# The last 256 tokens before the router: division and projection queued ahead of leftovers, gate logits from unnormalized rows

## The chip, the cores and the metric

The kernel runs on one core of a Trainium2 chip. A core has a matrix engine (TensorE, PE in the profile, with its weight loads as PEld), a vector engine (VectorE, DVE), a scalar engine (ScalarE, ACT), a general engine (GpSimd, POOL) and a queue that only issues transfers (SyncE, SP). Each engine takes its own instructions in the order in which they were queued and waits on semaphores for the others. The metric is the device time of one execution in microseconds (us), here the median of three runs. The profile is that of one further execution.

## The reference: what is computed

Four layers act on x, which holds 4 x 1024 tokens of 256 features. Each is wrapped as `x = x + layernorm(layer(layernorm(x)))`. The first is a gated attention unit with groups of 64 tokens, the second a low-rank feed-forward layer, the third an attention with 16 heads whose weights are `relu(scores)` divided by their row sum, and the fourth a mixture of experts. The change lies where the third ends and the fourth begins:

```python
# third layer, attention
w = relu(q @ k.T / 4);  out = (w / (sum(w) + 1e-6)) @ v
y = x + out @ w_out + b_out          # x here is the normalized input
attn = layernorm(y) * gamma + beta
x = x + layernorm(attn)
# fourth layer, experts: xt is layernorm(x), 4096 rows
S = sigmoid(xt @ Wg).T               # 8 experts x 4096 tokens
G, I = top_k(S, 1024)                # each expert picks its 1024 best tokens
hid = gelu(xt[I] @ W1 + b1)
out = (hid @ W2 + b2) * G            # added back to the chosen rows
```

An expert's choice needs the scores of all 4096 tokens. No expert can begin before the last token has left the attention and has its gate logit.

## The kernel before, in words

Tokens lie in eight blocks `xs[0..7]` of 512 (four tiles of 128 on the partitions). The attention loop (line 1634 on) goes over the batch rows, the query blocks `qh` of 512 tokens, and within these over head groups `g` and key tiles `kt`. For each step `scores` lets PE form `sc` (L1501), ACT and DVE turn it into `w` by a relu (L1509, L1513, L1511, L1517), and two steps later `weigh` lets PE accumulate `po` (L1529). The values carry a column of ones, so `po` holds the row sums too. The very last query block is taken in two halves of 256 tokens (`halves = 2`). The first 256 are called the other quarter below. The second 256 are the last tokens, whose `at_end` is true.

PE, DVE and ACT keep the order in which the program writes their instructions (`manual_schedule`). POOL's and SP's instructions are ordered by the planner of the framework. What follows the scores of a quarter (projection, layer norms, gate) is cut into `Part`s with costs and ages. Those on PE wait in the list `beside`, the others in `rest`, and `next_piece` and `go_on` queue them between the score steps. When the loop is done, four Parts of the other quarter are left. Two are in `rest`: `token_rows` of its two tiles, which normalizes a tile into `hg` (POOL, L1136) and stores `hg` to `tok_d` and x to `x_d` (L1333, L1337). Two are in `beside`: `turn_gating`, which transposes `hg` on PE (L1349) and copies it on ACT (L1352), and `gate`, which multiplies by the gate weights `wgp` (PE, L1364) and adds the result to `logits` (DVE, L1375).

In the kernel before, a loop (L1674) queues these four, and only then line 1683 queues the close of the last tokens, `at_once` (L1391). Its order is as follows. The first half of the projection (`pt`, L1288, channels 0). The transposes of all other tokens' `logits` into `tokens` (L1402). Three idle matmuls (`keep_busy`, L203: their result is not used). The division `by_weight` (DVE, L1257 to L1259) and the transpose `back` into `oT` (L1267). The second half of the projection, which needs `oT`, and 34 idle matmuls. DVE clips the other tokens' logits (L1413), ACT takes their exponential (L1419), and DVE adds the residual into y (L1421). Then there are three sets of moments on DVE with a power on POOL (`moments`, L1384 to L1388), between which y is centred, scaled and added to x (L1424, L1426, L1429, L1431). The normalized rows `hg` (DVE, L1435) are stored and transposed (L1349), copied (ACT, L1352), and multiplied by the gate weights (`pg`, L1364). DVE clips the logits (L1446), PE transposes them (L1449), and ACT takes the exponential (L1450). Meanwhile DVE finishes the sigmoid of the other tokens (L1440, L1441) and SP stores it (L1442).

The small PSUM tiles of this stage (`pt`, `tokens`, `tpg`, `pg`) share three buffers in turn (`side`), so that each new one waits until the third before it has been read.

The expert stage follows. POOL copies the known scores into `by_e` (L1701), DVE finishes the last tokens' sigmoid (L1702, L1703), POOL copies it back (L1704) and SP stores it (L1705). SP loads the bias `mb2` and the weights of two experts (L1707, L1714, L1716). ACT fills a table `each` (L1722) and loads the Gelu table by a tiny activation (L1727). A search for the threshold of expert 0 alternates between DVE (L1755, L1762, L1784, L1787) and PE (L1769). A list of its tokens is built (L1828 to L1918, with `each` read at L1894 and PE's L1904 collecting). POOL gathers the rows from `tok_d` (L1928), PE transposes them (L2098), and from then on PE works without pause on the experts (L2120, L2137).

## Time and profile before

| what | value |
|---|---|
| median of three runs | 1509.32 us (1509.0 to 1512.29) |
| profiled execution, time | 1511.89 us |
| profiled execution, span in the profile | 1510.1 us |
| mean granted PE clock | 0.985 |
| end of the last `po` matmuls | 970.63 us in the span |
| first use of the last tokens' scores (L1702) | 990.12 us |
| first expert matmul (L2120) | 1020.73 us |
| gather of expert 0 (first L1928) | 1015.40 us |

The difference of 1.8 us between time and span lies outside the span. The page of the profile gives, for each engine, its busy time, then its busy tenths in 40 slices of 37.75 us, and the clock that PE was granted. A line of the timeline has the start, the duration, the engine, the source line, the operation, the tile written and the tiles read, the shape, and the number of instructions merged. In brackets stands how long the engine was idle before it and which instruction ended that wait.

### The profile page before, as it was taken

The numbers are of one execution on the slowest core, as the hardware profiler recorded it, in microseconds if no ns is written. First come the engines' busy times: TensorE is split into PE (matmuls) and PEld (weight loads), VectorE is DVE, ScalarE is ACT, GpSimd is POOL, SyncE is SP. The second block draws the span as 40 slices with busy tenths as digits, with TensorE's granted clock in tenths as the row PEclk, the third lists the DMA queues.
The fourth block names the chain that finished last, engine by engine and source line by source line (L and its number), as shares of the span: only waits on it lengthen the run. The fifth ranks groups of instructions, "written<-read, shape, count | busy, mean of one in ns | idle before, by whom it ended". The sixth has DMA issues, their size and how long they took to land. (4 is left out here: it accounts for less than half of the span.)

```text
span 1510.1 us, 24181 instructions
## 1 busy us (share of the span) xinstructions
PE 1461.7 (97%) x9286; PEld 786.1 (52%) x9286; DVE 876.1 (58%) x2140; ACT 698.2 (46%) x1148; POOL 496.5 (33%) x627
## 2 busy tenths in 40 slices
PE   8999999999899999999999999949999999999996
PEld 4666666667532333332333335517666656665674
DVE  5456654666356599659974877775545631322145
ACT  4244455443456666767676788612211122112143
POOL 4123332222350214322432233413334243242554
PEclk9999999999999999999999999969999999999998
DMA  9400000003324141533154210241324324233364
GB/s 219 132 1 1 1 1 1 1 0 101 103 93 144 52 135 60 179 102 102 47 174 140 71 57 30 75 133 34 101 54 92 67 53 98 50 78 81 64 171 122
DMA packets 91885, 121.58 MB, mean 81 GB/s; under 512 B 24925, under 2 KB 64250, under 8 KB 91642
## 3 DMA queue, kind: packets, MB, share of 16 engines
q1 hardware_dynamic: 70000, 73.09, 15.4%
q0 software_dynamic: 21712, 46.94, 13.3%
q8 instruction: 73, 1.20, 0.3%
q14 instruction: 42, 0.34, 0.1%
q10 hardware_dynamic: 58, 0.01, 0.0%
HBM read 66.90 MB, written 53.12 MB: 79 GB/s over the span
## 5 line engine op out<-in xcount | busy, mean ns | idle before, releaser
L1529 PE MATMUL po<-w,vaug 128*17 128x512 f32 (+1 forms) x2304 | 270.1, 551 | 2.8 <-DVE turned L1579 2.6
L2127 ACT ACTIVATE hid<-ph,mb 128x512 f32<-128x512 f32 (+1 forms) x136 | 89.9, 662 | 340.4 <-PE ph L2120 247.8
L2120 PE MATMUL ph<-xT,w 128*128 128x512 f32 (+1 forms) x544 | 229.6, 574 | 0.3 <-DVE xT L2103 0.3
L2137 PE MATMUL py<-w,hid 128*128 128x256 f32 x1024 | 229.7, 380 | 0.0
L2137 PEld LDWEIGHTS py<-w,hid 128*128 128x128 f32 x1024 | 191.7, 190 | 31.7 <-issue 6.7
L1517 DVE TENSOR_SCALAR w<-sc 128x1024 f32<-128x1024 f32 x152 | 185.1, 1222 | 36.2 <-PE sc L1501 33.8
L1509 ACT ACTIVATE w<-sc 128x512 f32<-128x512 f32 x256 | 152.9, 597 | 113.7 <-ACT w L1513 49.5
L1501 PE MATMUL sc<-q,kT 32*128 32x512 f32 (+1 forms) x2304 | 190.8, 413 | 2.2 <-ACT w L1509 1.0
L1501 PEld LDWEIGHTS sc<-q,kT 32*128 32x128 f32 x2304 | 86.2, 183 | 174.7 <-ACT w L1509 92.1
L2158 POOL DMA_INDIRECT acc_d<-y,idx x56 | 88.8, 1586 | 225.2 <-DVE y L2157 103.2
L2120 PEld LDWEIGHTS ph<-xT,w 128*128 128x128 f32 x544 | 99.8, 190 | 107.4 <-issue 98.3
L1513 ACT ACTIVATE w<-sc 128x512 f32<-128x512 f32 x203 | 120.2, 592 | 0.0
L1515 ACT ACTIVATE w<-sc 128x1024 f32<-128x1024 f32 x104 | 106.7, 1026 | 0.0
L2156 DVE TENSOR_TENSOR y<-py,mb 128x256 f32<-128x256 f32 x56 | 23.5, 420 | 126.7 <-PE py L2137 116.1
L1529 PEld LDWEIGHTS po<-w,vaug 128*17 128x17 f32 x2304 | 41.7, 95 | 95.8 <-issue 72.3
L1928 POOL DMA_INDIRECT got<-tok_d,idx x64 | 66.6, 1041 | 62.9 <-DVE counts L1762 24.5
L2103 DVE COPY xT<-tp 128x512 f32<-128x512 f32 (+1 forms) x34 | 22.2, 659 | 71.1 <-PE tp L2098 62.4
L724 PE MATMUL pg<-nT,wh 128*128 128x512 f32 x128 | 61.4, 612 | 1.5 <-ACT nT L663 1.5
L850 PE MATMUL py<-wo,oT 128*128 128x256 f32 x256 | 61.9, 385 | 0.0
L740 PE MATMUL pv<-wh,nT 128*128 128x512 f32 x128 | 59.7, 592 | 0.0
L850 PEld LDWEIGHTS py<-wo,oT 128*128 128x128 f32 x256 | 47.2, 190 | 17.2 <-issue 9.6
L915 ACT ACTIVATE hid<-ph,vec 128x512 f32<-128x512 f32 x64 | 39.8, 685 | 27.5 <-PE ph L906 27.4
(309 smaller groups left out, 2108.8 us busy)
## 6 DMA issues: line engine op xcount, KB each, us to landing
q<-q_d POOLq DMA_DIRECT2D x16, 1024.0 KB
w<-in_L_ffn_W_dram SPq DMA_DIRECT2D x16, 1024.0 KB
q_d<-parts SPq DMA_DIRECT2D x48, 256.0 KB
kT<-k_d POOLq DMA_DIRECT2D x16, 512.0 KB
k_d<-parts SPq DMA_DIRECT2D x24, 256.0 KB
acc_d<-logits SPq DMA_DIRECT2D x8, 512.0 KB
tok_d<-hg SPq DMA_DIRECT2D x32, 128.0 KB
x<-in_L_attn_x_dram SPq DMA_DIRECT2D x7, 512.0 KB
```

Source lines behind the costliest of these rows:

```text
L850: nc.tensor.matmul(py, lhsT=d["oT"][:, e, :], rhs=wo[:, e, :], start=(e == 0), stop=(e == EC - 1))
L1501: nc.tensor.matmul(sc[:, m * n : (m + 1) * n], lhsT=row["kT"][t][rows, r, (kt + m) * P : (kt + m + 1) * P], rhs=row["q"][qh, t][rows, r, p ...
L1509: nc.scalar.activation(w[:, 0, :], singles[0], AF.Relu)
L1513: nc.scalar.activation(w[:, 1, :], singles[1], AF.Relu)
L1515: nc.scalar.activation(w[:, 2:4, :], pair, AF.Relu)
L1517: nc.vector.tensor_scalar(w[:, 2:4, :], pair, 0.0, None, ALU.max)
L1529: nc.tensor.matmul(po[32 * j : 32 * j + HD + 1, weighed(halves, r)], lhsT=row["v"][:, kt + m, HQ * t + 4 * r + j, :], rhs=w[:, j, m * n : ...
L1928: return nc.gpsimd.indirect_dma_start(out=dst, out_offset=None, in_=rows[:, :], in_offset=self.at_chunk(c), bounds_check=NT - 1, oob_is_er ...
L2120: nc.tensor.matmul(ph, lhsT=w1[:, c, f * P : (f + 1) * P], rhs=xT[u][:, c, h * n : (h + 1) * n], start=(c == 0), stop=(c == DC - 1),)
L2127: nc.scalar.activation(hid[:, f, h * n : (h + 1) * n], ph, AF.Gelu, bias=mb1[:, e * FC + f : e * FC + f + 1])
L2137: nc.tensor.matmul(py, lhsT=hid[:, f, i * P : (i + 1) * P], rhs=w2[:, f, :], start=(f == 0), stop=(f == FC - 1),)
L2158: scatter = nc.gpsimd.indirect_dma_start(out=acc_d[:, :], out_offset=lists[e].at_chunk(k), in_=y, in_offset=None, bounds_check=NT - 1, oob ...
```

## The change

1. The loop that queued the leftovers becomes a function `go_on_down_to(n)`, which is handed to `at_once`. It is called with 1 behind the division and the transpose of the last tokens (this queues both `token_rows` and `turn_gating` of the other quarter), and with 0 behind the first set of moments (this queues its `gate`). So the first half of the projection stands in PE's queue ahead of the other quarter's transposes, and the division stands in DVE's queue ahead of the other quarter's logit sum.
2. The transposes of the other tokens' logits, the clip and the exponential move behind that. The idle matmuls change from 3 and 34 to 2 and 20, and their places change.
3. The gate of the last tokens no longer takes the normalized rows. x itself is transposed and multiplied by the gate weights, and ACT copies the product out. A matmul of a tile of ones with the gate weights gives the column sums of the weights on every partition (`of_gate`). After the transposes of the logits, DVE forms `(of_gate * mean - logit) * rs`, clips it at 87 and hands it to the exponential, now without a scale of -1. This is the logit of the normalized rows with its sign turned.
4. The normalized rows are still written to `tok_d`, but POOL forms them, and they are queued behind the exponential.
5. `each` and the Gelu table are made to wait for the last exponential.

```diff
@@ -1339,15 +1339,16 @@
             def token_rows_and_on(i, rs, ms):
                 token_rows(i, lambda dst, src: scaled(dst, src, rs, ms))
 
-            def turn_gating(i0):
+            def turn_gating(i0, of=None):
                 if i0 == tiles[0]:
                     new_turn([] if at_end else [*turns, gates])
                     gating["hT"] = wk.tile([P, DC, TB], F32, tag="hT", name="hTg")
+                of = gating["h"] if of is None else of
                 tp = side([P, DC, 2, P], "tpg")
                 for c in range(DC):
                     for i in range(2):
                         nc.tensor.transpose(
-                            tp[:, c, i, :], gating["h"][:, i0 + i, c * P : (c + 1) * P], ident
+                            tp[:, c, i, :], of[:, i0 + i, c * P : (c + 1) * P], ident
                         )
                 nc.scalar.copy(
                     gating["hT"][:, :, i0 * P : (i0 + 2) * P], tp.rearrange("p c i t -> p c (i t)")
@@ -1388,68 +1389,80 @@
                     nc.gpsimd.tensor_tensor(rs[:, :, 0], ve[:, :, 0], mhalf[:, 0:2], ALU.pow)
                 return [(i, mv[:, k, 0:1], rs[:, k, :]) for k, i in enumerate(tiles)]
 
-            def at_once(by_weight, back):
+            def at_once(by_weight, back, go_on_down_to):
 
 
                 new_y()
                 x, stt = xs[t], nc.vector.scalar_tensor_tensor
+                k_tiles = SEG // P
                 pts = [(i, side([P, D], "pt")) for i in tiles]
                 for i, pt in pts:
                     project_tile(pt, i, (0,))
-                idle = ps.tile([P, 2, TB], F32, tag="d", name="idle", bufs=2)[:, 0, :]
-                tokens = side([P, SEG // P, P], "tokens")
-                for k in range(SEG // P):
-                    nc.tensor.transpose(tokens[:, k, :], logits[:, k * P : (k + 1) * P], ident)
-                keep_busy(idle, 3)
                 by_weight()
                 back()
+                go_on_down_to(1)
                 for i, pt in pts:
                     project_tile(pt, i, (1,))
-                keep_busy(idle, 34)
-
-
-                for k in range(SEG // P):
-
-                    nc.vector.tensor_scalar(
-                        score_t.rearrange("p (b z k) e -> p k z b e", b=B, k=SEG // P)[:, k],
-                        tokens[:, k, :].rearrange("p (z b e) -> p z b e", b=B, e=NE),
-                        -87.0, None, ALU.max,
-                    )
-                known = score_t[:, 0 : NTILE - SEG // P]
-                nc.scalar.activation(known, known, AF.Exp, scale=-1.0)
+
+                idle, psum = (ps.tile([P, 2, TB], F32, tag="d", name=name, bufs=2)[:, 0, :] for name in ("idle", "psum"))
+                ones = wk.tile([P, P], F32, tag="parts", name="ones")
+                nc.gpsimd.memset(ones, 1.0)
+                of_gate = wk.tile([P, NE], F32, tag="parts", name="of_gate")
+                keep_busy(idle, 2)
                 for i, pt in pts:
                     nc.vector.tensor_tensor(y[:, i, :], pt, h[:, i, :], ALU.add)
                 scales = moments("b", y, "take")
+                go_on_down_to(0)
+                tokens = side([P, k_tiles, P], "tokens")
+                for k in range(k_tiles):
+                    nc.tensor.transpose(tokens[:, k, :], logits[:, k * P : (k + 1) * P], ident)
+                for c in range(DC):
+                    nc.tensor.matmul(psum[:, 0:NE], lhsT=ones, rhs=wgp[:, c, 0, 0:NE], start=(c == 0), stop=(c == DC - 1))
+                nc.scalar.copy(of_gate, psum[:, 0:NE])
+                keep_busy(idle, 20)
                 for i, mean, rs in scales:
                     stt(y[:, i, :], y[:, i, :], mean, gam, ALU.subtract, ALU.mult)
                 for i, mean, rs in scales:
                     stt(y[:, i, :], y[:, i, :], rs, bet, ALU.mult, ALU.add)
                 scales = moments("c", y, "take")
+
+                for k in range(k_tiles):
+
+                    nc.vector.tensor_scalar(
+                        score_t.rearrange("p (b z k) e -> p k z b e", b=B, k=k_tiles)[:, k],
+                        tokens[:, k, :].rearrange("p (z b e) -> p z b e", b=B, e=NE),
+                        -87.0, None, ALU.max,
+                    )
+                known = score_t[:, 0 : NTILE - k_tiles]
+                nc.scalar.activation(known, known, AF.Exp, scale=-1.0)
                 for i, mean, rs in scales:
                     nc.vector.tensor_scalar(y[:, i, :], y[:, i, :], mean, None, ALU.subtract)
                 for i, mean, rs in scales:
                     stt(x[:, i, :], y[:, i, :], rs, x[:, i, :], ALU.mult, ALU.add)
-                for i, mean, rs in moments("g", x, "take"):
+                turn_gating(tiles[0], x)
+                pg, rows = gate()
+                scales = moments("g", x, "take")
+                nc.vector.tensor_scalar(known, known, 1.0, None, ALU.add)
+                nc.vector.reciprocal(known, known)
+                nc.sync.dma_start(score_rows[:, 0 : NTILE - k_tiles], known)
+                last_logits = wk.tile([P, SEG], F32, tag="hT", name="last_logits")
+                nc.scalar.copy(last_logits[rows, :], pg[rows, :])
+                tokens = side([P, k_tiles, 32], "tokens")
+                for k in range(k_tiles):
+                    nc.tensor.transpose(tokens[:, k, :], last_logits[rows, k * P : (k + 1) * P], ident[rows, rows])
+                at = wk.tile([P, k_tiles, NE], F32, tag="even", name="at", bufs=1)
+                for k, (i, mean, rs) in enumerate(scales):
+                    stt(at[:, k, :], of_gate, mean, tokens[:, k, 32 - NE : 32], ALU.mult, ALU.subtract)
+                for k, (i, mean, rs) in enumerate(scales):
+                    nc.vector.tensor_scalar(at[:, k, :], at[:, k, :], rs, 87.0, ALU.mult, ALU.min)
+                state["exp"] = nc.scalar.activation(score_t[:, NTILE - k_tiles : NTILE], at, AF.Exp)
+                for i, mean, rs in scales:
                     token_rows(
                         i,
-                        lambda dst, src, mean=mean, rs=rs: nc.vector.tensor_scalar(
+                        lambda dst, src, mean=mean, rs=rs: nc.gpsimd.tensor_scalar(
                             dst, src, mean, rs, ALU.subtract, ALU.mult
                         ),
                     )
-                turn_gating(tiles[0])
-                nc.vector.tensor_scalar(known, known, 1.0, None, ALU.add)
-                nc.vector.reciprocal(known, known)
-                nc.sync.dma_start(score_rows[:, 0 : NTILE - SEG // P], known)
-
-                pg, rows = gate()
-                last_logits = wk.tile([P, SEG], F32, tag="hT", name="last_logits")
-                nc.vector.tensor_scalar(last_logits[rows, :], pg[rows, :], -87.0, None, ALU.max)
-                tokens = side([P, SEG // P, 32], "tokens")
-                for k in range(SEG // P):
-                    nc.tensor.transpose(tokens[:, k, :], last_logits[rows, k * P : (k + 1) * P], ident[rows, rows])
-                nc.scalar.activation(
-                    score_t[:, NTILE - SEG // P : NTILE], tokens[:, :, 32 - NE : 32], AF.Exp, scale=-1.0
-                )
 
             gating = {}
             if at_end:
@@ -1671,16 +1684,20 @@
             row = after
         while waiting:
             finish(*waiting.pop(0))
-        while beside or rest:
-            Part.now += 1
-            assert Part.now < 2000
-            late[:] = [-2.0, -2.0, -2.0]
-            piece = next_piece()
-            if piece is not None:
-                beside.remove(piece)
-                piece()
-            go_on()
-        state["close"][0](*divide(state, DC - 1))
+
+        def go_on_down_to(n):
+
+            while len(beside) > n or rest:
+                Part.now += 1
+                assert Part.now < 2000
+                late[:] = [-2.0, -2.0, -2.0]
+                piece = next_piece()
+                if piece is not None:
+                    beside.remove(piece)
+                    piece()
+                go_on()
+
+        state["close"][0](*divide(state, DC - 1), go_on_down_to)
     both.close()
 
 
@@ -1719,12 +1736,15 @@
         weights = [load_expert(0), load_expert(1)]
 
         each = keep.tile([P, P, NTILE], BF16, name="each")
-        nc.scalar.activation(each, count_p.unsqueeze(2).to_broadcast([P, P, NTILE]), AF.Copy, scale=-1.0 / P)
+        behind_exp = mybir.DependencyInfo(mybir.DependencyClass.Sync, mybir.DependencyReason.DATA)
+        whole = nc.scalar.activation(each, count_p.unsqueeze(2).to_broadcast([P, P, NTILE]), AF.Copy, scale=-1.0 / P)
+        tc.add_manual_dep(whole.ins, state["exp"].ins.name, behind_exp, reason="the last scores go ahead")
 
         whole_c = keep.tile([P, NC], F32, name="whole_c")
         nc.gpsimd.tensor_scalar(whole_c, count_c, LARGE, None, ALU.add)
 
-        nc.scalar.activation(spare, spare, AF.Gelu)
+        loaded = nc.scalar.activation(spare, spare, AF.Gelu)
+        tc.add_manual_dep(loaded.ins, state["exp"].ins.name, behind_exp, reason="the last scores go ahead")
 
         sums = keep.tile([P, 2, NTILE + 1], F32, name="sums")
         nc.gpsimd.memset(sums, 0.0)
```

## Prediction

> **What bounds the kernel now.** I read the page first, then the chain that ended last around the change, then the timelines of DVE and PE there, and last the clock in stretches of 1 us. The page:
>
> ```profile
> span 1510.1 us, 24181 instructions
> PE 1461.7 (97%) x9286; PEld 786.1 (52%) x9286; DVE 876.1 (58%) x2140; ACT 698.2 (46%) x1148; POOL 496.5 (33%) x627
> PEclk9999999999999999999999999969999999999998
> ```
>
> PE is busy nearly everywhere, and only one slice inside the run has a low clock (6 tenths, 981 to 1019 us). There PE's work is idle matmuls and waits: from the last `po` at 970.63 to the first expert matmul at 1020.73 one serial chain runs through all engines. What shortens that chain brings every later matmul forward. DVE's timeline, with some lines left out:
>
> ```profile
> 970.70 0.45 DVE L1579 STREAM_TRANSPOSE turned<-po 128x256 f32<-128x256 f32 x1 [1.13 <-PE po L1529]
> 973.77 0.42 DVE L1375 TENSOR_TENSOR logits<-logits,pg 32x256 f32<-32x256 f32 x1 [2.63 <-PE pg L1364]
> 974.22 0.17 DVE L1257 TENSOR_SCALAR den<-turned 128x16 f32<-128x16 f32 x1
> ...
> 975.18 0.45 DVE L1267 STREAM_TRANSPOSE oT<-even 128x256 f32<-128x256 f32 x1
> 975.65 0.49 DVE L1413 TENSOR_SCALAR logits<-tokens 128x128 f32<-128x128 f32 x2
> 976.41 0.86 DVE L1421 TENSOR_TENSOR y<-pt,h 128x256 f32<-128x256 f32 x2 [0.27 <-PE pt L1288]
> ...
> 985.00 0.74 DVE L1435 TENSOR_SCALAR hg<-x,mvg,rsg 128x256 f32<-128x256 f32 x2 [0.87 <-POOL rsg L1388]
> 985.65 0.28 DVE L1440 TENSOR_SCALAR logits<-logits 128x240 f32<-128x240 f32 x1
> 985.96 1.65 DVE L1441 RECIPROCAL logits<-logits 128x240 f32<-128x240 f32 x1
> 988.96 0.43 DVE L1446 TENSOR_SCALAR last_logits<-pg 32x256 f32<-32x256 f32 x1 [1.35 <-PE pg L1364]
> 990.12 0.18 DVE L1702 TENSOR_SCALAR by_e<-logits 128x16 f32<-128x16 f32 x1 [0.73 <-ACT logits L1450]
> ```
>
> The division (L1257) has its input at 971.15 but stands behind L1375, which waits 2.63 us for the other quarter's gate. At the end DVE waits for the transposed and gated `hg`. PE's side:
>
> ```profile
> 971.46 0.55 PE L1349 MATMUL tpg<-ident,hg 128*128 128x128 f32 x3 [0.58 <-POOL hg L1136]
> 972.68 1.05 PE L1364 MATMUL pg<-hTg,wgp 128*32 128x256 f32 x4 [0.68 <-ACT hTg L1352]
> ...
> 976.64 7.50 PE L203 MATMUL idle<-all_b 128*128 128x512 bf16 x34
> 985.56 0.78 PE L1349 MATMUL tpg<-ident,hg 128*128 128x128 f32 x4 [1.41 <-DVE hg L1435]
> 987.01 1.92 PE L1364 MATMUL pg<-hTg,wgp 128*32 128x256 f32 x4 [0.67 <-ACT hTg L1352]
> ```
>
> The same four `pg` instructions take 1.05 us the first time and 1.92 the second. The clock in stretches says why (the third number from the end is the granted clock):
>
> ```profile
> 985.00:986.00 1.00, 0.44 (x3) 0.35 (x4) 0.97 (x4) 0.00 (x0) 0.00 (x0) 1.00 0.00 0
> 986.00:987.00 1.00, 0.34 (x3) 0.10 (x1) 1.00 (x1) 0.61 (x2) 0.00 (x0) 0.79 0.63 210
> 987.00:988.00 1.00, 0.99 (x3) 0.49 (x4) 0.61 (x1) 1.00 (x1) 0.32 (x1) 0.50 0.88 261
> ```
>
> **The change part by part.** T is the start of the first L1421 (976.41 before).
>
> *Division ahead.* L1257 follows `turned` at once: in the half before, `turned` started at 957.60 and L1257 at 958.08, so here at 971.18 instead of 974.22. L1257 to the end of L1267 takes 1.40 us, then comes 0.05 to PE and 0.73 to L1421. PE is free in time: first half of `pt` 970.6 to 971.6, the four `tpg` from then (the second `hg` ends at 971.42) to about 972.3, while `oT` comes at 972.6. T is 973.37: **3.04 us earlier**.
>
> *What DVE gets in between.* L1375 (0.42) now follows the first moments. It hides partly behind the power `rsb` on POOL (978.44 to 979.34), for which DVE waited 0.23 us; cost 0.15 to 0.2. Its `pg` needs a buffer read by the first L1421, so it runs from about 974.1 to 975.2, just when DVE gets there. The two clips L1413 (0.49) fall into the wait for `rsc` (0.32 idle): cost 0.2. So x is complete at about 980.35 (before, 983.04).
>
> *PE's queue to the transposes of x.* `tokens` waits for L1375 (ends 975.64): 0.5 us for two transposes, to 976.15. The four instructions for `of_gate` have no row; nearest is a float32 weight load, 190 ns, so 4 x 0.19 = 0.76 at most, 0.3 if loads overlap; I take 0.5. ACT's copy of 128x8 (the 128x16 exponential took 0.18) stands free. Twenty idle matmuls at the old rate, (7.50 - 0.38)/33 = 0.216 us, are 4.32: to about 980.97. So the idle matmuls, not DVE, end last, by 0.6 us; DVE may be that much late at no cost.
>
> *From there to the scores.* Four transposes in a row 0.62 (the chain shows 0.59 for such a group in the loop), copy L1352 0.59, `pg` 1.09 with its hand-over (972.68 to 973.77), ACT's copy of 32x256 out of PSUM 0.37 (between the 0.27 of the 128x128 cast L1913 and the 0.58 of a 128x512 copy) against 0.43 on DVE, transposes 0.45 as before. Then four small DVE operations for `at`: L1257-like ones start every 0.21, so 0.8. Exponential to L1702 0.22 plus 0.05. Sum from 980.97: 0.62 + 0.59 + 1.09 + 0.37 + 0.45 + 0.8 + 0.27 and 0.15 for three more hand-overs make 4.34, so L1702 starts at **985.3 instead of 990.12: 4.8 us earlier**.
>
> *The clock's share.* That sum has the second `pg` at full clock, 0.87 us cheaper. In the trace the clock fell at about 986.6, 2.4 us after the idle matmuls, with gaps of only 1.41 and 0.67 us in between. Now `pg` starts about 1.3 us after the last idle matmul. The Trainium skill, TensorE: Matmul & The Clock Gate, section Part 1, has the clock fall only after at least one idle window of some 3.4 us. By that rule the gaps before were too short to cool PE, the 1.92 has another cause, and it can return: 3.9. The row shows the clock itself at 0.50, so I go by the row. But windows of a fixed length need not lie alike in each execution: the profiled one is 2.6 us above the median, and the cheaper executions may have had a warm `pg` already. I give the median half of the 0.87: **4.4 us**.
>
> *DVE's other work.* The moments of x end about 981.5, L1440 and L1441 (1.93) by 983.4; `at` begins about 984.2. Cover 0.8 us; were it gone, each us late would count in full. L1701 (POOL, 0.60) then ends by 984.0 and is wanted at about 986 (L1755).
>
> *`hg` on POOL.* Two operations of 0.549 (L1136), off the path, since x itself is transposed. On POOL they pass nothing that is waited for, unless they go ahead of L1701 (2 us of cover). The three stores (two `tok_d`, one `x_d`; 0.3 to 0.45 of issue each on SP) stand ahead of or behind L1442 and the weight loads L1716 and L1714. The gather reads `tok_d` at 1015.40, some 1011 afterwards, and the transfers of the weights end by 1002 in the trace: over 10 us of cover for all; without it, late weights would stop PE at the first L2120. The skill's SBUF — State Buffer, section Who interferes with whom, speaks against the move: a DVE instruction with two SBUF inputs and a GpSimd one that reads SBUF take turns, the second waiting for the whole of the first. By the rule one small operation could stand 0.55 us behind an `hg`; by the row, L1136 took 0.548 to 0.631 in 54 uses beside a busy DVE, so at most 0.1. I take nothing and keep 0.55 for the range.
>
> *`each`, table loads.* 3.62 + 1.28 + 0.20 us on ACT move behind the exponential, ending about 990.5; L1894 wants `each` at 1010.42, some 1006 afterwards: 15 us of cover. The loads of the Exp table at 986.98 and of Gelu at 1014.04 (1.28 each) go away; ACT waited 1.65 and 6.58 us behind them, so nothing is won.
>
> *Behind L1702* the search, list and gather are the same chain and shift as they are; the clock window may fall elsewhere in it. In the trace the 16 idle matmuls at 1014 to 1019 ran half cold, and the gathered rows came 0.26 us after them: bounds -0.3 and +2 us.
>
> The profiled execution becomes 1511.89 - 4.8 = 1507.1, and the median 1509.32 - 4.4 = **1504.9**.
>
> **Rivals.** *Part is given back* (gain 1.5 to 3.5, 1506.8): a wait in the new stretch, such as L1375 late for `pg`, or the collecting matmuls L1904 and idle matmuls behind them at half clock (2.46 us for 31 would be near twice that). For it: these ran at a clock of 0.93 and 0.59. Against it: slacks of 0.6 and 0.8 on both sides. *Hidden anyway* (1509.3): the 20 idle matmuls run cold, 20 x 0.43 = 8.6 instead of 4.3, and take the gain. Against it: PE is busy over three quarters of the time from 970 to 976. *More than summed* (gain over 5.5, 1503.3): the later stretch at 1014 also stays warm. *Slower*: the ones for `of_gate` are filled by POOL, whose order the planner sets. If that memset stands behind the power `rsg` (about 982.2), PE's `of_gate` and all behind it wait until 982.3 instead of 976.15, 6.1 us: the gain of 4.8 becomes a loss of 1.3, 1510.6. It decides from 4.8 us of delay on; behind `rsc` (979.2) it costs 3.0 and leaves 1.8. Against it: it depends on nothing, and the planner put POOL's independent memsets L1730 and L1746 ahead of the power `rsb`.
>
> **How the numbers follow.** As summed (gain 3.8 to 5.5): 0.62. Part given back: 0.22, a third of it still over 3.0 us. Hidden: 0.05. More: 0.06. Slower: 0.05. 0.2% of the time, about what a measurement can tell here, is 3.0 us. So faster 0.62 + 0.06 + 0.07 = 0.75, within 0.19, slower 0.06. The likeliest case has 1503.8 to 1505.5; the range, with half of the cases of loss and the clock's bounds, is 1502.6 to 1508.2.
>
> **What would show it.** Right: L1257 within 0.1 us of the end of `turned`; L1421 at about 973.4; twenty idle matmuls that end at about 981 with x done before; the second `pg` near 1.05 us at a clock of 1.00; the step that was L1702 at about 985.3; the first expert matmul at about 1016. Wrong: DVE waiting at L1375 or ahead of `at`, idle matmuls that start after 978, a `pg` of 1.9, or a first expert matmul that moved less than the scores did.

## The result and the profile after

The changed kernel takes 1507.33 us (median of 20 runs, 1504.84 to 1510.84) beside 1509.16 us of the kernel before (20 runs of the same chip): a ratio of 0.9985, interval 0.9978 to 0.9992. By the medians that is 1.8 us less, where 4.4 were forecast. The ratio is not that of the two medians: it stands for 2.3 us, its interval for 1.2 to 3.3. The forecast range holds the measured time, the likeliest case's own range (1503.8 to 1505.5) does not. Nor did the outcome with the chance of 0.75 come, faster by more than 3.0 us: both figures lie in "within", which had 0.19. The profiled execution took 1510.32 us, 1.57 less than that of before (1511.89). Executions of every kernel here fall into clusters some 3 us apart, so a median can lie in either; the ratio's interval and the times inside the trace are the better guides.

The page's first lines (span, busy time by engine, and the clock in 40 slices):

```profile
span 1508.6 us, 24159 instructions
...
PE 1456.6 (97%) x9275; PEld 784.4 (52%) x9275; DVE 875.2 (58%) x2141; ACT 696.1 (46%) x1148; POOL 498.1 (33%) x630
...
PEclk9999999999999999999999999969999999999998
```

PE lost 11 instructions (15 idle matmuls fewer, four for `of_gate` more) and 5.1 busy us. At this scale little else differs; the change is seen only inside the slice with the low clock. DVE's timeline there:

```profile
972.10 0.45 DVE L1592 STREAM_TRANSPOSE turned<-po 128x256 f32<-128x256 f32 x1 [1.13 <-PE po L1542]
972.58 0.26 DVE L1257 TENSOR_SCALAR den<-turned 128x16 f32<-128x16 f32 x1
...
974.85 0.86 DVE L1413 TENSOR_TENSOR y<-pt,h 128x256 f32<-128x256 f32 x2 [0.79 <-PE pt L1288]
...
976.82 0.42 DVE L1376 TENSOR_TENSOR logits<-logits,pg 32x256 f32<-32x256 f32 x1
...
980.98 0.88 DVE L1441 SCALAR_TENSOR_TENSOR x<-y,rsc,x 128x256 f32<-128x256 f32 x2
...
986.62 0.29 DVE L1719 TENSOR_SCALAR by_e<-logits 128x16 f32<-128x16 f32 x1 [0.28 <-ACT logits L1458]
...
988.45 0.39 DVE L1775 TENSOR_TENSOR ge<-by_e,bits 128x224 bf16<-128x224 f32 x1 [1.25 <-DMA tok_d<-hg]
```

In this execution the last `po` ended at 972.03, 1.40 us later than in the trace of before (970.63), for a reason that lies ahead of the change (the clock, see the second trace of before). So all times below count from the end of the last `po`. The division follows `turned` at once, the waiting L1376 (L1375 before) no longer has a wait in front of it, and the scores (L1719, L1702 before) start at 14.59 instead of 19.49: 4.90 us earlier, with 4.8 summed. But the next step, `ge`, the first comparison of the threshold search, has a wait that was not there: 1.25 us on a store of `hg`. PE's timeline:

```profile
977.93 4.48 PE L203 MATMUL idle<-all_b 128*128 128x512 bf16 x20
982.25 0.60 PE L1350 MATMUL tpg<-ident,x 128*128 128x128 f32 x4
983.52 1.05 PE L1365 MATMUL pg<-hTg,wgp 128*32 128x256 f32 x4 [0.68 <-ACT hTg L1353]
```

The transposes of x, which stand behind the 20 idle matmuls, began at 10.22 (the ends of matmuls are modelled, so the two records overlap a little). x was complete at 9.83, and the second `pg` ran at full clock: 1.05 us, and the granted clock fell only at 14.3. The chain that ended last, from the third power of POOL on:

```profile
983.09 0.69 POOL rsg L1389
983.78 0.10 issue
983.89 2.44 POOL hg L1462 x2
986.33 0.02 issue
986.34 1.79 DMA tok_d<-hg
...
988.45 0.40 DVE ge L1775
```

The gate with its scores has left the chain. The way now leads through the two `hg` that the change moved to POOL, and through their store.

### The profile page after: what moved, and what is told of

It is laid out like the page before. It is cut to its first block, busy times and chain, and to the rows that moved or that the text cites. A ratio compares the mean times of both kernels' runs of the same rounds, so it can differ in the third digit from the quotient of the medians.

```text
span 1508.6 us, 24159 instructions
## 1 busy us (share of the span) xinstructions
PE 1456.6 (97%) x9275; PEld 784.4 (52%) x9275; DVE 875.2 (58%) x2141; ACT 696.1 (46%) x1148; POOL 498.1 (33%) x630
```

## The experiments

Times from the end of the last `po`, in us. "pg" is the duration of the last four instructions of that name.

| kernel | x complete | pg | scores | `ge` | first expert matmul | median (runs) | ratio to before |
|---|---|---|---|---|---|---|---|
| before | 12.42 | 1.92 | 19.49 | 20.15 | 50.11 | 1509.16 (20) | |
| second_before | 12.44 | 1.05 | 18.55 | 19.20 | 49.07 | 1508.37 (1) | |
| changed | 9.83 | 1.05 | 14.59 | 16.42 | 46.52 | 1507.33 (20) | 0.9985 [0.9978, 0.9992] |
| rep_after | 9.84 | 1.05 | 14.62 | 16.44 | 46.52 | 1508.66 (14) | 0.9991 [0.9980, 1.0002] |
| order_alone | 9.84 | 1.05 | 15.94 | 17.22 | 47.10 | 1507.63 (22) | 0.9988 [0.9978, 0.9997] |
| raw_gate_alone | 12.56 | 1.05 | 17.35 | 19.14 | 49.22 | 1509.30 (14) | 0.9996 [0.9984, 1.0007] |
| hg_other_form | 9.86 | 1.05 | 14.45 | 19.95 | 50.02 | 1511.46 (15) | 1.0018 [1.0009, 1.0027] |
| hg_other_memory | 9.84 | 1.05 | 14.61 | 15.40 | 45.47 | 1506.80 (22) | 0.9984 [0.9975, 0.9993] |
| hg_on_dve_and_memory | 9.86 | 1.05 | 14.49 | 15.17 | 44.93 | 1507.38 (14) | 0.9986 [0.9977, 0.9995] |
| both_on_pool | 9.84 | 1.05 | 14.42 | 15.10 | 45.13 | 1506.93 (22) | 0.9980 [0.9971, 0.9989] |
| idle_6 | 9.84 | 1.05 | 14.42 | 15.10 | 45.15 | 1504.57 (12) | 0.9969 [0.9955, 0.9982] |
| copy_on_act_6 | 9.84 | 1.91 | 14.97 | 15.65 | 45.72 | 1508.07 (15) | 0.9974 [0.9963, 0.9984] |
| copy_on_act_20 | 9.84 | 1.05 | 14.39 | 15.07 | 45.12 | 1507.88 (15) | 0.9983 [0.9973, 0.9993] |
| copy_on_act_18 | 9.84 | 1.05 | 14.00 | 14.68 | 44.72 | 1506.97 (22) | 0.9983 [0.9975, 0.9991] |

My theory after the first comparison: the two `hg` on POOL in the form (subtract, multiply) are slow, `ge` has to wait until their stores have read them, because the expert stage takes over the memory of `hg`, and so the gate's gain stops there. The rivals: it is only the form of the operation; or the store is a bystander and the scores decide; or the forecast sum was wrong further up.

### The changed kernel once more: rep_after

No edit.

> The changed kernel once more, for a second trace beside the variants. From the end of the last po matmuls to the first expert matmul the first trace had 46.5 us (50.1 before the change). Theory: that stretch is the same within 0.3 us in every execution, and what differs between traces lies elsewhere (the clock at the start of the attention, 423 to 430 us, cost the first trace 1.40 us more than the trace of before). Rival: the change itself makes the attention slower; then the last po ends near 972.0 again, not 970.6, in every trace of it. Time: ratio to before 0.9985.

The stretch repeats (46.52 both times). The time does not: its ratio of 0.9991 has an interval that includes no change. What varies between these two executions lies outside the stretch. The last `po` ended at 970.94 here, so the rival that the change slows the attention is out.

### Another form of hg on POOL: hg_other_form

```diff
-  lambda dst, src, mean=mean, rs=rs: nc.gpsimd.tensor_scalar(
-      dst, src, mean, rs, ALU.subtract, ALU.mult),
+  ms = small.tile([P, 1], F32, tag="msg", name="msg")
+  nc.gpsimd.tensor_scalar(ms, mean, rs, -1.0, ALU.mult, ALU.mult)
+  lambda dst, src, rs=rs, ms=ms: scaled(dst, src, rs, ms)   # multiply, add
```

> The two normalized tiles still on POOL, but in the form of L1136 (times the scale, plus a shift that POOL forms first in two operations of 0.27). Theory: the form of the operation sets its 1.218 us, so it falls to 0.55, the tiles are done 0.8 us sooner (985.5 in the first trace's time), the store lands sooner, and the first ge of the search starts about 1.0 us sooner; stretch 45.5, ratio to before 0.9978. Rival: POOL is slowed by the reciprocal that runs on DVE beside it; then the two stay near 1.2 us each and the stretch grows by the 0.5 us of the two added operations, 47.0.

The form is what made `hg` slow. The groups of the two forms, POOL in the changed kernel:

```profile
L1462 POOL TENSOR_SCALAR hg<-x,mvg,rsg x2: 1215/1218/1221, 983.9 to 985.1; 128x256 f32<-128x256 f32 x2
```

and in the kernel before, where both forms stand (numbers: least, median and most ns of one, then the first and last start):

```profile
L592 POOL TENSOR_SCALAR y<-y,mvg,rsg x4: 1216/1218/1237, 422.7 to 426.3; 128x256 f32<-128x256 f32 x4
...
L1136 POOL TENSOR_SCALAR hg<-x,rsg,msg x30: 548/549/631, 567.1 to 970.9; 128x256 f32<-128x256 f32 x30
```

The same shape costs 1.218 us as (subtract, multiply) and 0.549 as (multiply, add); in hg_other_form both `hg` took 0.55. With the second form POOL was done early, and yet the kernel became slower than before. The reason is in SP's timeline, first that of the changed kernel, then that of hg_other_form, with its first `ge` (DVE's timeline) after it:

```profile
985.13 1.54 SPq L1333 DMA_DIRECT2D tok_d<-hg  x2
...
987.25 0.61 SPq L1447 DMA_DIRECT2D tok_d<-logits  x1
```

```profile
984.04 0.37 SPq L1447 DMA_DIRECT2D tok_d<-logits  x1
984.50 3.66 SPq L1333 DMA_DIRECT2D tok_d<-hg  x2
```

```profile
991.16 0.39 DVE L1772 TENSOR_TENSOR ge<-by_e,bits 128x224 bf16<-128x224 f32 x1 [5.04 <-DMA tok_d<-hg]
```

The planner, which orders SP, had put the store of the 240 known scores (L1447) ahead of the two stores of `hg`. One by one, these took 3.18 and 0.38 us to issue. In the changed kernel they took 0.34 and 0.33 (the 1.54 of the line is mostly SP's wait for the second `hg`), and there the store next behind L1447, that of the last scores (L1722), took 4.85, which nothing waited for. `ge` stood 5.04 us for the stores of `hg`, and the scores, 0.14 us earlier than in the changed kernel, gained nothing by it. The total was a miss of my expectation. The stretch of 50.02 is at most 0.95 us longer than before (49.07 in the second trace of before), so the ratio, some 2.7 us, is not all explained by it. It speaks for the theory all the more: an early or late store of `hg` moves `ge`, whatever the scores do.

### The same form in other memory: hg_other_memory

```diff
-  hg = gating["h"][:, i, :]
+  hg = wq1[:, i - tiles[0], :] if at_end else gating["h"][:, i, :]
```

> The two normalized tiles are written into the memory of wq1, which nobody reads any more and which the expert stage does not take over; POOL's operations stay as they are. Theory: the first ge waits for the stores of hg because the expert stage's pool lies on hg's memory; without that it starts when by_e is there, about 987.4 instead of 988.45 in the first trace's time, 1.05 us sooner; stretch 45.5, ratio 0.9978. Rival: it is POOL's copy of by_e behind the two slow operations that the search waits for; then nothing moves, 46.5.

`hg` is written over the query weights, which nothing reads any more, and POOL's two slow operations stay. DVE's timeline:

```profile
986.11 0.28 DVE L1719 TENSOR_SCALAR by_e<-logits 128x16 f32<-128x16 f32 x1 [0.28 <-ACT logits L1458]
...
986.90 0.39 DVE L1775 TENSOR_TENSOR ge<-by_e,bits 128x224 bf16<-128x224 f32 x1 [0.22 <-DVE by_e L1720]
```

The wait on the store is gone, `ge` follows the scores after 0.79 us, and the first expert matmul comes at 45.47 as expected: 1.05 us less than in the changed kernel. POOL and SP work as before (the stores of `hg` start at 13.12 and 14.33, in the changed kernel at 13.10 and 14.31). This settles the wait. It was not the data of `hg` that `ge` needed but the memory. In the built program `ge` waits on the semaphores of the last two stores of `hg`. `ge` itself lies elsewhere: it is the first tile of a pool that, as a whole, covers memory of the attention stage, that of `hg` included.

### hg on DVE, ahead of the gate's last steps, and the other memory: hg_on_dve_and_memory

```diff
+  for i, mean, rs in scales:                       # moved up, ahead of `at`
+      token_rows(i, lambda ...: nc.vector.tensor_scalar(dst, src, mean, rs, ALU.subtract, ALU.mult))
   at = wk.tile([P, k_tiles, NE], F32, tag="even", name="at", bufs=1)
...
-      nc.gpsimd.tensor_scalar(...)                 # after the exponential
```

> The two normalized tiles on DVE, between the reciprocal and the small operations for the last scores (0.74 us, where DVE waited 0.62), and in the memory of wq1. Theory: neither POOL nor a store stands ahead of the search, and the small DVE operations that POOL's hg held up (L1457 0.45 instead of 0.23, L1719 0.29 instead of 0.18) are short again: ge starts about 1.4 us sooner than in the changed kernel, stretch 45.1, ratio 0.9975. Rival: DVE's 0.74 us push the scores back by what they exceed the wait, and the search waits for something else: 46.0 or more.

At 44.93 within 0.2 of what was expected. Moving `hg` from DVE to POOL had not been needed: on DVE both cost 0.93 us in a place where DVE waits for the transposes, and the scores came no later (14.49).

### Each half of the change by itself: order_alone and raw_gate_alone

```diff
 # order_alone: go_on_down_to and the new order as in the change; the gate as before
-  turn_gating(tiles[0], x)        # of_gate, at and hg on POOL left out
+  for i, mean, rs in moments("g", x, "take"):
+      token_rows(i, lambda ...: nc.vector.tensor_scalar(..., ALU.subtract, ALU.mult))
+  turn_gating(tiles[0])
-  keep_busy(idle, 20)
+  keep_busy(idle, 28)
```

```diff
 # raw_gate_alone: everything of the other quarter queued first, as before
+  go_on_down_to(0)
   state["close"][0](*divide(state, DC - 1), go_on_down_to)
-  keep_busy(idle, 20)
+  keep_busy(idle, 28)
```

> Only the order is taken over: division and projection ahead of the other quarter's leftovers, with 28 idle matmuls; the gate still takes the normalized rows and `hg` stays on DVE. Times from the end of the last `po`. If the whole of the gain that the changed kernel kept is that of the order, and its gate brings next to nothing because `ge` waits for the store of `hg`: x complete at 9.6 to 9.8 (before 12.42), scores at about 16.6 (before 19.49), `ge` at about 17.2, first expert matmul at 47.1 (before 50.11, changed 46.52), so a gain of 2.9 to 3.0 us against 3.6 of the whole change. If the gate carries its share as predicted (1.8 of 4.8), the first expert matmul is at 48.3.

> Only the gate from raw rows is taken over, with `hg` on POOL; the leftovers of the other quarter stay ahead of the division, and 28 idle matmuls fill the longer wait. Times from the end of the last `po`. x complete at 12.4 as before, scores at about 17.2 (2.3 earlier than before). If the store of `hg` decides, `ge` comes 6.6 after x as in the changed kernel, at 19.0 (before 20.15), and the first expert matmul at 49.1 to 49.4 (before 50.11): a gain of 0.7 to 1.0 us. If the scores decide, as the prediction had it, `ge` is at 17.9 and the first expert matmul at 48.1, a gain of 2.0.

Both first expert matmuls came where the theory of the store had them (47.10 and 49.22). For order_alone that is luck: the scores came at 15.94, 0.66 earlier than expected (`pg` took 1.05 us, not 1.92), and a wait for the store that I had not expected took 0.62 of it back. Even with the old gate the store binds once the division is early; DVE's timeline of order_alone, then of raw_gate_alone:

```profile
984.43 0.18 DVE L1706 TENSOR_SCALAR by_e<-logits 128x16 f32<-128x16 f32 x1 [0.62 <-ACT logits L1451]
984.64 0.25 DVE L1707 RECIPROCAL by_e<-by_e 128x16 f32<-128x16 f32 x1
985.71 0.39 DVE L1759 TENSOR_TENSOR ge<-by_e,bits 128x224 bf16<-128x224 f32 x1 [0.82 <-DMA tok_d<-hg]
```

```profile
984.05 0.26 DVE L1720 TENSOR_SCALAR by_e<-logits 128x16 f32<-128x16 f32 x1 [0.29 <-ACT logits L1458]
...
985.84 0.39 DVE L1776 TENSOR_TENSOR ge<-by_e,bits 128x224 bf16<-128x224 f32 x1 [1.24 <-DMA tok_d<-hg]
```

By their times the order alone brings nearly all (0.9988 beside 0.9985), and the gate alone nothing that can be told from no change (0.9996, interval 0.9984 to 1.0007), although it has the scores at 17.35 instead of 19.49.

### The kernel before, a second trace: second_before

No edit.

> The kernel before once more, for a second trace: the stretch from the last `po` to the first expert matmul is 50.1 again if the second `pg` is at half clock again, and 49.2 (0.87 less) if the windows in which the clock is granted lie so that the clock is still full there; the last `po` ends within 4 us of 970.6.

The stretch was 49.07 this time, 1.04 less. PE's timeline, and the clock in stretches of 1 us (the third number from the end is the granted clock):

```profile
983.19 0.78 PE L1349 MATMUL tpg<-ident,hg 128*128 128x128 f32 x4 [1.41 <-DVE hg L1435]
984.64 1.05 PE L1364 MATMUL pg<-hTg,wgp 128*32 128x256 f32 x4 [0.68 <-ACT hTg L1352]
```

```profile
985.00:986.00 1.00, 0.69 (x4) 0.11 (x1) 0.52 (x2) 0.89 (x1) 0.60 (x1) 1.00 0.97 277
986.00:987.00 1.00, 0.31 (x2) 0.20 (x2) 0.35 (x3) 0.18 (x1) 0.00 (x0) 1.00 0.88 191
987.00:988.00 1.00, 0.00 (x0) 0.00 (x0) 0.78 (x3) 0.00 (x0) 0.21 (x1) 0.65 1.00 350
```

The same idle gaps (1.41 and 0.68 us), the same work, and a `pg` of 1.05 us instead of 1.92: the clock fell at 19.1 from the end of `po` here, at 16.0 in the first trace. The records of the granted clock show why. Within each execution all its falls lie on one grid of 3.413 us (in the first trace 396.1, 423.4, 986.6, 1013.9 and 1502.0, whole multiples apart), and from one execution to the next the grid lies differently against the program. So the stretch of before is 50.11 in one execution and 49.07 in another, and the change's gain in it is 3.59 or 2.55 us.

In every other kernel of the table but copy_on_act_6 `pg` took 1.05 us, so this second trace is the fair one to compare them with. Beside it order_alone gains 1.97 us in the stretch, raw_gate_alone loses 0.15, and the whole change gains 2.55. raw_gate_alone has the scores 1.20 us earlier (18.55 to 17.35) and `ge` only 0.06: the wait for the store takes it all.

The same grid goes with what happens ahead of the change. Between 395 and 430 us, at the start of the attention, the traces have different numbers of windows of 3.413 us at a granted clock of 0.50, and the last `po` ends the later the more there are: none, at 966.69 us (raw_gate_alone); one, at 968.23 to 968.49 (four traces); three, at 970.63 to 971.01 (three); four, at 971.20 to 972.05 (six). The first trace of before had three, that of the changed kernel four; its repetition had three and second_before one, so the number is not the kernel's. No run changed it on purpose.

### What the idle matmuls and the last shared port cost: both_on_pool, idle_6, and copy_on_act with 6, 20 and 18

both_on_pool takes the edits of hg_other_form and hg_other_memory together. idle_6 is that with `keep_busy(idle, 6)` for 20. The three copy_on_act kernels add

```diff
-  nc.gpsimd.tensor_copy(by_e[:, :, known], score_t[:, known].rearrange("p j e -> p e j"))
+  nc.scalar.copy(by_e[:, :, known], score_t[:, known].rearrange("p j e -> p e j"))
```

with 6, 20 and 18 idle matmuls.

> The whole change, with `hg` on POOL in the multiply-add form and in the memory of the query weights. The two single edits gave 50.02 (form, the store came late) and 45.47 (memory). If the memory alone frees `ge` from the store, the form now only frees POOL 1.3 us earlier for the copy of the scores: `ge` at 14.9 to 15.2 from the end of the last `po`, first expert matmul at 44.9 to 45.2, although the store of the scores goes ahead of the stores of `hg` again. If the late stores still count (through the gather of the rows), it stays at 46 or more.

> As both_on_pool, with 6 idle matmuls instead of 20, so that PE has nothing to do for some 2.6 us before the transposes of x. If short gaps are enough to let the clock fall, as the trace of before showed after gaps of 1.41 and 0.67 us: the second `pg` takes 1.9 us instead of 1.05 and the transposes more than 0.7, the scores come 0.5 to 1.0 later, first expert matmul at 45.4 to 46.1. If only a whole idle window of 3.4 us cools PE: `pg` stays at 1.05, the transposes start 0.35 earlier, first expert matmul at 44.6 to 44.9.

both_on_pool is a hit (45.13): in other memory the late store harms nothing. idle_6 shows `pg` at 1.05 after a gap of 2.13 us, and PE 0.38 us earlier, yet the scores at the same 14.42. That half was a miss. Groups of the two last steps of `at` on DVE in both_on_pool, then in idle_6, where also POOL's copy of the known scores is shown:

```profile
L1457 DVE TENSOR_SCALAR at<-at,rsg x2: 218/244/271, 982.2 to 982.4; 128x8 f32<-128x8 f32 x2
```

```profile
L1457 DVE TENSOR_SCALAR at<-at,rsg x2: 219/436/652, 981.8 to 982.4; 128x8 f32<-128x8 f32 x2
...
L1715 POOL COPY by_e<-logits x1: 607/607/607, 981.9 to 981.9; 128x240 f32<-128x240 f32 x1
```

An operation on eight columns took 652 ns and ended 29 ns after POOL's copy. The 0.38 us that PE had won were lost in it. The long ones in other traces end the same way, 25 to 30 ns behind a POOL operation: 447 ns in the changed kernel and 460 in raw_gate_alone behind `hg`, 271 in both_on_pool behind the copy.

> As idle_6, with the copy of the 240 known scores (L1715 there, 0.607 us on POOL) on ACT behind the exponential. Times from the end of the last `po`. In idle_6 the second L1457 took 652 ns instead of 219 and ended when POOL's copy had ended. If the two share one port, and that ate the 0.38 us that PE had won: both L1457 at about 220 ns, scores at 14.0 (idle_6: 14.42), `ge` at 14.65 to 14.75 (15.10), first expert matmul at 44.7 to 44.8 (45.15). If something else made L1457 long, it stays near 650 ns and the scores at 14.4; if ACT's copy (about 0.4) comes too late, `ge` stays at 15.0 or more.

> As both_on_pool with 20 idle matmuls, and the copy of the known scores on ACT. POOL's copy met only the first L1457 there (271 ns instead of 219), so little is to be won by the port: scores at 14.3 to 14.4 (14.42), first expert matmul at 45.0 to 45.1 (45.13). Beside copy_on_act_6 it prices the 0.35 us by which the 20 idle matmuls end after x: 0.35 if nothing else hides it.

> Everything that the earlier runs showed to help, in one kernel: the whole change, `hg` on POOL in the multiply-add form and in the memory of the query weights, the copy of the known scores on ACT, and 18 idle matmuls, which should end at about 9.8 from the end of the last `po`, just when x is complete (20 ended at 10.2, 6 let the second `pg` run at half clock in one execution of two). If PE's late idle matmuls and POOL's copy were each hiding the other's price: transposes of x at about 9.9, second `pg` 1.05 us long, ending at 12.2, scores at 14.0 to 14.05 (copy_on_act_20: 14.39), `ge` at 14.7, first expert matmul at 44.7 to 44.8 (45.12). If PE is not what binds, the scores stay at 14.4. In time some 0.4 us less than both_on_pool, which is within what runs can tell, and 4.4 to 5.4 less than before in the stretch.

With the copy on ACT the two L1457 took 231 and 225 ns, so POOL it was. But copy_on_act_6 has the scores at 14.97, because the clock's grid lay otherwise in that execution:

```profile
981.55 0.94 PE L1350 MATMUL tpg<-ident,x 128*128 128x128 f32 x4 [2.13 <-DVE x L1441]
983.17 1.91 PE L1365 MATMUL pg<-hTg,wgp 128*32 128x256 f32 x4 [0.68 <-ACT hTg L1353]
```

Six idle matmuls leave `pg` to chance: 1.05 us once, 1.91 once, after the same gap. Twenty end 0.4 us after x. Eighteen fit, DVE's and PE's lines of copy_on_act_18:

```profile
984.36 0.36 DVE L1457 TENSOR_SCALAR at<-at,rsg 128x8 f32<-128x8 f32 x2
...
985.01 0.18 DVE L1716 TENSOR_SCALAR by_e<-logits 128x16 f32<-128x16 f32 x1 [0.28 <-ACT logits L1458]
...
985.69 0.39 DVE L1772 TENSOR_TENSOR ge<-by_e,bits 128x224 bf16<-128x224 f32 x1 [0.21 <-DVE by_e L1717]
```

```profile
980.81 0.65 PE L1350 MATMUL tpg<-ident,x 128*128 128x128 f32 x4
982.13 1.05 PE L1365 MATMUL pg<-hTg,wgp 128*32 128x256 f32 x4 [0.67 <-ACT hTg L1353]
```

Scores at 14.00, `ge` at 14.68, first expert matmul at 44.72, all as expected. Each of the last two edits alone had brought nothing (45.15 with 6 idle matmuls, 45.12 with the copy), since each hid what the other costs. The stretch is 1.80 us shorter than in the changed kernel. In time that cannot be told apart: 0.9983 [0.9975, 0.9991] beside 0.9985. It is the version with the shortest stretch; that it beats the changed kernel in time is not shown. idle_6 has the lowest ratio (0.9969), but its stretch equals that of both_on_pool (0.9980); where the difference comes from is not shown.

## Why the prediction was partly right

**The bound** was read rightly: one serial chain from the last `po` to the first expert matmul. A shift at its `ge` goes through: from `ge` to the first expert matmul the changed kernel needs 30.10 us, that of before 29.96.

**Division ahead**: 3.04 forecast, T from 5.79 to 2.83 is 2.96. x complete was forecast 2.69 earlier and came 2.59 earlier (12.42 to 9.83). L1376, the clips and the pieces on PE cost what was said.

**PE's queue**: the idle matmuls end last, forecast by 0.6 us, measured by 0.39. **From there to the scores**: forecast 4.34, measured 4.37 (982.25 to 986.62). So the scores came 4.90 us earlier beside the 4.8 of the sum. Of both, some 0.9 is the clock: beside the second trace of before they came 3.96 earlier, and the sum without its 0.87 for the clock says 3.93.

**The step that failed** is the paragraph "`hg` on POOL": "Two operations of 0.549 (L1136), off the path, since x itself is transposed." Both halves were wrong. The size came from a row of another pair of operations. L592 stood in the same profile, has the same pair, and says 1.218. And they are not off the path. The place that I followed was the data (`hg` to `tok_d` to the gather at 1015, 10 us of cover); the memory was not asked about. The pool of the first `ge` takes over what the stores of `hg` still have to read. The kernel before has the same memory, but there no wait for a store shows ahead of `ge` (0.19 us idle, behind `by_e`), since its scores came later; with the division early and `hg` still on DVE, order_alone waits. In the sum: `ge` stood 0.66 us behind the start of the scores before and 1.83 after, 1.17 us lost. hg_other_memory gives 1.05 of it back at the first expert matmul. It is also the sign of being wrong that the forecast named: the first expert matmul moved less (3.59) than the scores (4.90).

**Behind the scores** another 0.31 us went between `ge` and the first `kept` (1.12 us before, 1.43 after), and 0.17 came back up to the first expert matmul. The 0.31 is a longer idle gap of DVE ahead of `kept`; DVE's timeline of before, then of the changed kernel:

```profile
991.90 0.23 DVE L1784 SCALAR_TENSOR_TENSOR kept<-parts,grown 128x64 f32<-128x64 f32 x1 [0.18 <-PE parts L1769]
```

```profile
989.88 0.22 DVE L1804 SCALAR_TENSOR_TENSOR kept<-parts,grown 128x64 f32<-128x64 f32 x1 [0.48 <-PE parts L1789]
```

The view names PE's `parts`, but these had ended 0.34 us earlier in the changed kernel, 0.04 in that of before. The longer gap is there in every kernel with `hg` on POOL and in none with `hg` on DVE. Its cause stays open. Sum: 4.90 - 1.17 - 0.31 + 0.17 = 3.59, as measured (50.11 to 46.52).

**The shared pair of ports**: I weighed the rule of the Trainium skill (SBUF — State Buffer, Who interferes with whom), took the row, and put it at nothing. The rule was the better guide, though not by the sentence that I took from it: L1457 has one tile and a per-partition scalar, not two input tiles, and the same section counts `tensor_scalar` among the operations that can take both ports. In the changed kernel the second L1457 took 447 ns beside 231 for the first, ending with POOL's `hg`, and the scores' step L1719 0.29 instead of 0.18 beside POOL's copy. That is 0.33 us, of which 0.22 lies inside the sum up to the scores, made up elsewhere in it by luck, and it is within the 0.55 kept as its bound. L1136's 54 uses showed what POOL suffers, not what a small DVE operation suffers beside it. `at`'s first step, with one input in PSUM, was not slowed (215 to 221 ns each beside POOL's `hg` in the changed kernel, and the same in copy_on_act_6 with POOL idle), as the rule has it for a single SBUF input.

**The clock's share**: the choice of the row over the rule, and of half its 0.87 for the median, was right in kind. The page of the Trainium skill that the forecast cites, TensorE: Matmul & The Clock Gate, section Part 1, calls the window of 3413 ns free-running, and the second trace of before shows just that: falls whole multiples of 3.413 us apart, and `pg` of 1.92 or 1.05 by where the grid lies. Its idle window needs a gloss: the one that ended with the fall at 986.6 held 1.72 us of PE work (0.94 of idle matmuls, 0.78 of transposes), so it need not be empty. How busy it may be the runs do not settle (see the last section). At the scores the warm case is worth 0.94 us, at the first expert matmul 1.04. How often the kernel before is cold was not counted.

**`each`, table loads, the ones for `of_gate`**: hidden, as said. POOL filled the ones early, so the rival on the slower side did not occur. A rival of that kind exists nevertheless, in a place where I did not look: in hg_other_form, 0.18% above the kernel before, the order of the stores on SP took back what the earlier scores had won in the stretch.

**The whole**: of the stretch's 3.59 us the profiled execution shows 1.57. The last `po` came 1.40 later, ahead of the change; from the first expert matmul to the last `py` it was 0.32 shorter; and the end, from the start of the last `py`, was 0.96 longer (12.12 to 13.08), because the scatters into `out_dram` wait for a store there. In the repetition the chain has that as its own line:

```profile
1482.32 4.93 DMA out_dram<-x
1488.19 1.16 POOL out_dram L2052
```

3.59 - 1.40 + 0.32 - 0.96 is 1.55. That end took 12.1 to 12.3 us in seven of the traces (both of before, order_alone, raw_gate_alone, hg_other_memory, idle_6, copy_on_act_6) and 13.0 to 13.6 in the other seven, both of the changed kernel among them. In these seven the first of the scatters waits for that store, in the others it does not. No edit separates the two groups; why the store lands later in some stays open. It leaves the measured gain (1.8 us by the medians, 1.2 to 3.3 by the ratio's interval) in keeping with a stretch gain of 2.55 to 3.59 less up to 1 us.

So the case that came true is the rival *part is given back* (gain 1.5 to 3.5, 1506.8): the size fits, its place does not. It named L1375, the collecting matmuls or the idle ones. It was a pool laid over memory that a store had not finished reading.

## What to carry to other kernels

When a step is moved behind the critical result because its data are wanted late, ask also who takes over its memory and when; a buffer that is read by a late store holds up the first tile of the next stage. Cost an operation by a row with the same pair of operations on the same engine, not by one of the same shape. Where two small costs hide each other (PE's filler and a port on DVE), an edit that removes one shows nothing: remove both before giving either up.

## What the runs showed of the hardware

- A POOL tensor_scalar on 128x256 float32 with two pointers took 1.218 us as (subtract, multiply) and 0.549 us as (multiply, add).
- The granted clock fell from 1.00 to 0.50 on a grid of 3.413 us that is fixed within an execution and lies differently in each. How much of a window PE was busy does not settle whether it falls: a fall after 0.51 in the first trace of before, none after 0.51 and 0.56 in idle_6, and another fall in the first trace of before, at 1013.9, after a window that PE's records (small collecting matmuls, L1904) cover to 0.80.
- The more windows at half clock at the start of the attention (none to four), the later the last `po` ended: 966.69 to 972.05 us in the 14 traces, over 5 us for kernels whose edits lie behind it.
- A DVE operation of 8 columns took 652 ns instead of 219 beside a POOL copy of 607 ns, ending 29 ns after it, and 225 to 231 ns when that copy ran on ACT.
- Behind a store of 120 KB of scores on SP, the next store took 3.18 us to issue (`hg` in hg_other_form, 0.34 without) or 4.85 (the last scores, in the changed kernel).
